# A two-block transformer/Mamba kernel: half of a causal convolution moves from VectorE to TensorE in the last two sequences, with two small moves beside it

## The chip, the cores and the metric

The kernel runs on one core of a Trainium2 chip. The metric is the time of one execution on the device, in microseconds (us). Several executions are timed and the median is taken. One execution is also recorded by the hardware profiler, and all readings below come from that record. TensorE is called PE (PEld is its weight load), VectorE DVE, ScalarE ACT, GpSimd POOL and SyncE SP.

## The reference, cut to what matters

Two blocks run one after the other on an input of 4 sequences, 256 tokens and 512 features, in float32. The first is attention plus a gated feed-forward network. The second normalizes and then adds a selective scan (Mamba) and a mixture of low-rank experts. The change touches the Mamba part only (`d` is one of 1024 channels, `n` one of 16 states):

```python
x, z = split(hidden @ in_proj_w)              # each [b, l, d], transposed to [b, d, l]
xc = conv_b + sum(conv_w[:, k] * xpad[:, :, k : k + 256] for k in range(4))
xc = silu(xc)
dt, B, C = projections of xc, each through an rmsnorm; dt also through softplus
h[t] = exp(dt[t] * A) * h[t-1] + dt[t] * B[t] * xc[t]      # per channel and state
y[t] = sum over n of h[t, n] * C[t, n]
out = ((y + D * xc) * silu(z)) @ out_proj_w
```

## The kernel before

**Layout.** Channels lie on the 128 partitions, so 1024 channels are 8 chunks of 128. Chunks are handled in pairs (`p` = 0 to 3), a pair's two products filling one PSUM tile of 2 x 256 float32 called `px`. The 16 states of a chunk are taken four at a time: one "unit" of the scan stage is 4 states of one chunk, laid out as 128 x 1024: 32 channels x 4 states on the partitions, and 4 such groups of 256 time steps side by side. There are 4 units to a chunk, 32 to a sequence and 128 in all.

**A unit.** In program order unit `u` does: `decays(u + 2)` on ACT, four exponentials of 128 x 255 (L888); then whatever the plan has put at unit `u`; `scan_in(u)` on DVE, the product `bx` (L894); now and then `close_chunk` on DVE, which reads the finished PSUM sum `ysum` of a chunk and multiplies it with the gate (L929); `scan(u)`, the recurrence `h` on DVE (L909) and after it the product `hc` of `h` with C on POOL (L913); and last `states_sum(u - 1)` on PE, which adds the states of the unit before into `ysum` (L923, L925). The last unit alone is scanned in four quarters (`parts=4`, L1277).

**Buffers that tie the engines together.** There are three decay tiles, so `decays(u + 2)` waits for `scan(u - 1)`. There are two `h` tiles, so `scan(u)` waits for the POOL product `hc(u - 2)`. There are three `hc` tiles, so `hc(u)` waits for `states_sum(u - 3)`. `ysum` is a single bank: `close_chunk` at the second unit of a chunk waits for the sum of the last unit of the chunk before. PSUM tiles named `mm` (three of them) hold `px`, the gates' products `pz`, the outputs `po` and small ones in turn.

**The plan.** The order is written out by hand: `put(b, s, f, ...)` (L1141) calls `f` at unit `s` of sequence `b`, and each engine runs its instructions in that order. While sequence `b` is scanned, the next sequence `nxt = b + 1` is prepared. For `nxt` = 2 and 3 the products `px_mm` of pair `p` stand at units 6 + 2p and 7 + 2p, `conv_in` at 8 + 2p, `conv_taps` at 9 + 2p, `conv_silu` at 16; for `nxt` = 1 all are one unit later (L1205 to L1218). After that come `pp_mm` and `pp_norm` (the projections, up to `nrm`, L754), `step_in` and `step_exp` (dt on PE and ACT) and `step_out`, `step_x` (POOL). The first sequence's own convolution stands ahead of the units (L1039 to L1061).

**The convolution before.** A convolution of four taps is a sum of four shifted products. `conv_in` (L699) copies `px` into a padded SBUF tile (L704, ACT) and starts both chunks with the last tap and the bias (L707, ACT: first chunk in place in `px`, second chunk into `xc`), then writes the other three taps of the second chunk (L712, ACT). `conv_taps` (L716) adds the first chunk's three taps on DVE (L720) and the second chunk's on POOL (L726):

```python
for k in range(KC - 1):
    nc.vector.scalar_tensor_tensor(
        px[:, 0, :] if k < KC - 2 else xcs[b][:, c, :], pads[p % 2][:, 0, k : k + S],
        vec[:, c, V_CW + k : V_CW + k + 1], px[:, 0, :], ALU.mult, ALU.add,
    )
```

**The gates of the first sequence.** `pz_mm` is four products into a half of `pz` (L857). For sequence 0, pair 1, both halves stand at unit 8 (L1173 to L1175).

Of the kernel before, what the change touches and what calls it, by code (L numbers as in the profile page):

```python
# [8 lines left out]
F32 = mybir.dt.float32  # L9

F32R = mybir.dt.float32r
AF = mybir.ActivationFunctionType
ALU = mybir.AluOpType
# [4 lines left out]
P = 128  # L18
B, S, D = 4, 256, 512
# [6 lines left out]
DIN, NST, KC, RK = 1024, 16, 4, 32  # L26
DC = DIN // P
NE, LR = 8, 16
NG = 4
# [8 lines left out]
V_CW, V_CB, V_DB, V_AL, V_D, V_END = 0, 4, 5, 6, 22, 23  # L38
# [3 lines left out]
def block_kernel(  # L42
# [655 lines left out]

    def conv_in(b, p):  # L699

        px = live["px", b, p]
        if p == 0:
            xcs[b] = (act if b % 3 else w1).tile([P, DC, S], F32, tag=f"xc{b % 3}", name="xc")
        nc.scalar.copy(pads[p % 2][:, :, KC - 1 :], px)  # L704
        for i in range(2):
            v = vec[:, 2 * p + i, :]
            nc.scalar.activation(xcs[b][:, 2 * p + 1, :] if i else px[:, 0, :], px[:, i, :],  # L707
                                 AF.Identity, bias=v[:, V_CB : V_CB + 1],
                                 scale=v[:, V_CW + KC - 1 : V_CW + KC])
        tp = w1.tile([P, KC - 1, S], F32, tag="tap", name="tap")  # L710
        for k in range(KC - 1):
            nc.scalar.activation(tp[:, k, :], pads[p % 2][:, 1, k : k + S], AF.Identity,  # L712
                                 scale=vec[:, 2 * p + 1, V_CW + k : V_CW + k + 1])
        live["tap"] = tp

    def conv_taps(b, p):  # L716

        px, c = live["px", b, p], 2 * p
        for k in range(KC - 1):
            nc.vector.scalar_tensor_tensor(  # L720
                px[:, 0, :] if k < KC - 2 else xcs[b][:, c, :], pads[p % 2][:, 0, k : k + S],
                vec[:, c, V_CW + k : V_CW + k + 1], px[:, 0, :], ALU.mult, ALU.add,
            )
        xc = xcs[b][:, c + 1, :]
        for k in range(KC - 1):
            nc.gpsimd.tensor_tensor(xc, xc, live["tap"][:, k, :], ALU.add)  # L726
# [172 lines left out]
    def scan(u, parts=1):  # L899
        b, c, g = u // PER, u % PER // NU, u % NU  # L900
        da, bx = live.pop(("da", u)), live["bx"]
        if u < len(lent["h"]):
            h, hc = lend("h", u), lend("hc", u)
        else:
            h = act.tile([P, NG, S], F32, tag="h", name="h", bufs=2)
            hc = act.tile([P, NG, S], F32, tag="hc", name="hc", bufs=3)
        for k in range(parts):
            n = slice(k * NG // parts, (k + 1) * NG // parts)
            nc.vector.tensor_tensor_scan(  # L909
                h[:, n].rearrange("p n t -> p (n t)"), da[:, n].rearrange("p n t -> p (n t)"),  # L910
                bx[:, n].rearrange("p n t -> p (n t)"), 0.0, ALU.mult, ALU.add,
            )
            nc.gpsimd.tensor_tensor(  # L913
                hc[:, n], h[:, n],
                crows[b][:, g, :].unsqueeze(1).to_broadcast([P, NG // parts, S]), ALU.mult,
            )
        live["hc", u] = hc
# [223 lines left out]
    def put(b, s, f, *a):  # L1141
        at.setdefault(b * PER + s, []).append((f, a))
# [5 lines left out]
    for b in range(B):  # L1148
        nxt = b + 1
        if b:  # L1150
            put(b, 0, b_rows, b, 1)
            put(b, 0, spread, "du", b, 1)

            for c in range(DC):
                put(b, c // 2, out_mm, b - 1, 1, c)
            put(b, 3, out_x, b - 1, 1)
            put(b, 4, dense, b - 1, 0, 0)
            put(b, 5, dense, b - 1, 0, 1)
            put(b, 5, expert_out, b - 1, 0)
            for c in range(DC):  # L1160
                put(b, 6 + c, out_mm, b - 1, 0, c)
            put(b, 15, out_x, b - 1, 0)
        else:
            put(b, 1, one_out, 2)
            put(b, 1, one_step, 3)
            put(b, 2, one_out, 3)
            put_late(b, 2, load_z, b, 0)
            put_late(b, 2, lambda: send("dt", 0, 1, dts[0, 0][:, 2:4, :]))
            put_late(b, 2, step_x, b, 1)
            put(b, 4, load_z, b, 1)  # L1170
            for k, n in enumerate(("rl", "bw", "lb", "ow")):
                put(b, 9 + 2 * k, load_late, n)
            for p, u in ((0, 3), (1, 8)):  # L1173
                for i in range(2):
                    put(b, u, pz_mm, b, p, i)  # L1175
            put(b, 4, gate_silu, b, 0)
            put(b, 12, gate_silu, b, 1)
            put_late(b, 1, add_last, 5)
            put_late(b, 3, add_last, 6)
            put_late(b, 4, add_last, 7)  # L1180
        if b:
            put(b, 0, gate_silu, b, 0, 1)

        o = 0 if b else 3
        put(b, 1 if b else 5, step_in, b, 1, 0)
        put(b, 2 if b else 6, step_in, b, 1, 1)
        put(b, 3 if b else 7, step_exp, b, 1)
        for q in range(2):
            for k in range(3):
                put(b, 5 + o + 3 * q + k, step_out, b, 1, q, k)  # L1190
        for p in (2, 3):
            put(b, 3 * p + 2 + o, step_x, b, p)
        for c in range(2, DC):
            o = 0 if b or c < 4 else 1
            put(b, 3 if c == 2 and not b else 4 * c - 6 + o, spread, "dt", b, c)
            put(b, 4 * c - 4 + o, spread, "du", b, c)
        put(b, 10, load_z, b, 2)
        put(b, 12, load_z, b, 3)
        for p, at_i, at_g in ((2, (14, 15), 16), (3, (19, 21), 23)):
            for i in range(2):  # L1200
                put(b, at_i[i], pz_mm, b, p, i)
            if p == 3 or nxt == B:
                put(b, at_g, gate_silu, b, p)
        if nxt < B:
            o = 0 if b else 1  # L1205
            put(b, 0 if b else 2, norm_stats, nxt)
            put(b, 2 if b else 4, norm_scale, nxt)
            put(b, 3 if b else 5, norm_turn, nxt, 0)
            (put if b else put_late)(b, 4 if b else 5, norm_copy, nxt, 0)
            put(b, 4 if b else 5, norm_turn, nxt, 1)  # L1210
            (put if b else put_late)(b, 5, norm_copy, nxt, 1)
            for p in range(NP):
                put(b, 2 * p if b else (5, 6, 9, 9)[p], load_x, nxt, p)
                for i in range(2):
                    put(b, 6 + o + 2 * p + i, px_mm, nxt, p, i)
                put(b, 8 + o + 2 * p, conv_in, nxt, p)
                put(b, 9 + o + 2 * p, conv_taps, nxt, p)
            put(b, 16 + o, conv_silu, nxt, (b, 2))  # L1218
            put(b, 17 + o, pp_mm, nxt, 0)
            put(b, 18, pp_mm, nxt, 1)  # L1220
            put(b, 19, pp_square, nxt)
            put_late(b, 20, pp_norm, nxt)
            put(b, 21, step_in, nxt, 0, 0)
            put(b, 22, step_in, nxt, 0, 1)
            put(b, 22, c_rows, nxt, 0)
            put(b, 23, step_exp, nxt, 0)
            put(b, 23, c_rows, nxt, 1)
            for q in range(2):
                for k in range(3):
                    put(b, 24 + 3 * q + k, step_out, nxt, 0, q, k)  # L1230
            put(b, 27, step_x, nxt, 0)
            put(b, 27, spread, "dt", nxt, 0)
            put(b, 29, spread, "du", nxt, 0)
            put(b, 30, step_x, nxt, 1)
            put(b, 30, b_rows, nxt, 0)
            put(b, 31, spread, "dt", nxt, 1)
            put(b, 23, load_z, nxt, 0)
            put(b, 25, load_z, nxt, 1)
            for k, u in enumerate((27, 28, 29, 31)):
                put(b, u, pz_mm, nxt, k // 2, k % 2)  # L1240
            if b % 2 == 0:
                for i, u in enumerate((16, 17, 18, 20)):
                    put(b, u, router, b, i)
                put(b, 22, route_exp, b)
                put(b, 24, route, b)
            put(b, 25, expert_turn, b)
            put(b, 25, dense, b, 1, 0)
            put(b, 26, dense, b, 1, 1)
            put(b, 27, expert_out, b, 1)
        else:  # L1250

            put(b, 12, expert_turn, b)
            put(b, 17, dense, b, 0, 0)
            put(b, 18, dense, b, 0, 1)
            put(b, 18, expert_out, b, 0)
            put(b, 20, dense, b, 1, 0)
            put(b, 21, dense, b, 1, 1)
            put(b, 21, expert_out, b, 1)
# [138 lines left out]
```

## Time and profile before

| what | value |
|---|---|
| time, median of 4 runs | 887.55 us (887.29 to 891.42) |
| the profiled execution's own time | 887.29 us |
| its span, first to last instruction | 885.5 us |
| busy: PE, DVE, ACT, POOL | 751.2, 685.5, 526.0, 489.9 us |
| DVE: recurrence `h` L909, product `bx` L894 | 288.0 us in 129, 157.6 us in 128 |
| DVE: taps L720 | 14.4 us in 30 and 7.2 us in 15 |
| POOL: `hc` L913, taps L726 | 301.9 us in 131, 32.7 us in 45 |
| PE: `px` L696, 256 instructions | 65.6 us, 405 ns each |

The page has one line per group of instructions: the line of the code, the engine, the operation, the tiles written and read, how often, the time busy and the idle time just before, with what ended it. The timeline gives single instructions (start, length), and windows give the busy time of every engine in a stretch. A matmul in float32 shows as two instructions. The time of an execution is some 2 us longer than its span (887.29 against 885.5); times in the timeline count from the span's start.

### The profile page before, as it was taken

To read this page: it belongs to the slowest core of one execution; us is meant where nothing else is said; L and a number is where in the kernel's file an instruction comes from. 1 tells how busy PE (TensorE), PEld (TensorE's weight loads), DVE (VectorE), ACT (ScalarE), POOL (GpSimd) and SP (SyncE) were. 2 spreads that over 40 slices of the span, in tenths; PEclk is the share of its full clock that TensorE was granted. 3 is DMA by queue.
4 is the path that set the end of the run, shared out by engine and by line. 5 is a ranking of instruction groups with operands and counts; after the bars stand their busy time and mean duration, and the time that the engine had idled before them with its cause. 6 is when DMAs were issued, how large, how long until landed. Compare 5 with 4: busy or idle time off the path is not lost.

```text
span 885.5 us, 10460 instructions
## 1 busy us (share of the span) xinstructions
PE 751.2 (85%) x3554; PEld 430.3 (49%) x3554; DVE 685.5 (77%) x675; ACT 526.0 (59%) x1009; POOL 489.9 (55%) x377
## 2 busy tenths in 40 slices
PE   5999989999989999997797798678898777967975
PEld 3675545667556576664453344334444443422421
DVE  4695553477565333878999999999999999999996
ACT  4225446312536437778777687776786795764561
POOL 4222222001223242748967879869789759797664
PEclk9999999999999999999996999888999889997998
DMA  6232242001112241365832545442546231436200
GB/s 214 60 95 72 72 119 71 13 1 36 48 48 72 72 116 26 96 175 169 238 97 60 155 131 142 109 122 68 167 120 178 78 101 52 129 93 174 77 24 24
DMA packets 67343, 86.67 MB, mean 98 GB/s; under 512 B 12077, under 2 KB 52025, under 8 KB 66906
## 3 DMA queue, kind: packets, MB, share of 16 engines
q1 hardware_dynamic: 57930, 67.12, 26.9%
q0 software_dynamic: 9072, 18.35, 7.5%
q8 instruction: 28, 0.46, 0.2%
q10 hardware_dynamic: 288, 0.52, 0.2%
q14 instruction: 25, 0.20, 0.1%
HBM read 66.58 MB, written 10.22 MB: 87 GB/s over the span
## 4 chain that ended last, share of the span: by engine, by line
PE 40%; DVE 35%; ACT 13%; issue 5%; POOL 4%; DMA 2%; SPq 0%; DVEq 0%; POOLq 0%; ACTq 0%
DVE h L909 20%; DVE bx L894 7%; ACT decay L888 6%; PE po L442 5%; PE pu L417 5%; PE pg L417 4%; PE sc L329 4%; PE av L371 3%; POOL hc L913 3%; PE scT L361 3%; PE pp L740 2%; PE po L1017 2%; PE pz L857 1%; ACT pe L363 1%; PE px L696 1%
## 5 line engine op out<-in xcount | busy, mean ns | idle before, releaser
L913 POOL TENSOR_TENSOR hc<-h,cr 128x1024 f32<-128x1024 f32 (+1 forms) x131 | 301.9, 2307 | 99.5 <-DVE h L909 80.7
L909 DVE TENSOR_TENSOR_SCAN h<-decay,bx 128x1024 f32<-128x1024 f32 (+1 forms) x129 | 288.0, 2234 | 15.6 <-PE po L442 3.9
L888 ACT ACTIVATE decay<-dts,aneg 128x255 f32<-128x255 f32 x504 | 213.5, 498 | 118.2 <-DVE h L909 107.9
L894 DVE TENSOR_TENSOR bx<-brow,dus 128x1024 f32<-128x1024 f32 x128 | 157.6, 1231 | 3.7
L925 PE MATMUL ysum<-hc,stack 128*32 128x256 f32 x1024 | 90.1, 420 | 82.1 <-POOL hc L913 81.6
L429 POOL TENSOR_TENSOR hlo<-g,hhi 128x512 fp32r<-128x512 f32 x28 | 36.1, 1290 | 150.0 <-ACT hhi L428 150.0
L331 DVE TENSOR_REDUCE mpl<-sc 128x4 f32<-128x1024 f32 x64 | 77.2, 1223 | 23.8 <-PE sc L329 23.5
L925 PEld LDWEIGHTS ysum<-hc,stack 128*32 128x32 f32 x1024 | 21.4, 112 | 145.2 <-POOL hc L913 128.1
L400 POOL DMA_DIRECT2D wgu<-in_wgu x56 | 31.2, 557 | 90.9 <-PE pg L417 80.2
L363 ACT ACTIVATE pe<-scT 128x1024 f32<-128x1024 f32 x64 | 62.8, 1023 | 30.1 <-PE scT L361 29.8
L1017 PE MATMUL po<-ow,xc 128*128 128x512 f32 x128 | 72.1, 673 | 2.2 <-DVE xc L929 2.2
L696 PE MATMUL px<-xn1T,w_in 128*128 128x256 f32 x256 | 65.6, 405 | 1.1 <-DMA w_in<-in_inx 1.0
L857 PE MATMUL pz<-xn1T,w_in 128*128 128x256 f32 x256 | 66.0, 404 | 0.0
L696 PEld LDWEIGHTS px<-xn1T,w_in 128*128 128x128 f32 x256 | 51.1, 203 | 20.3 <-issue 9.3
L425 DVE SCALAR_TENSOR_TENSOR g<-g,pg 128x512 f32<-128x512 f32 x28 | 19.2, 685 | 52.0 <-ACT g L424 52.0
L857 PEld LDWEIGHTS pz<-xn1T,w_in 128*128 128x128 f32 x256 | 47.8, 195 | 17.8 <-issue 11.2
L428 ACT CAST hhi<-g 128x512 fp32r<-128x512 f32 x28 | 17.3, 620 | 63.0 <-DVE g L427 62.7
L417 PE MATMUL pg<-xhi,wgu 128*128 128x512 f32 x112 | 46.7, 417 | 7.0 <-issue 4.4
L417 PE MATMUL pu<-xhi,wgu 128*128 128x512 f32 x112 | 47.7, 426 | 2.0 <-DMA wgu<-in_wgu 0.9
L442 PE MATMUL po<-wd,hhi 128*128 128x512 f32 x112 | 48.5, 433 | 0.0
L329 PE MATMUL sc<-km,qg 128*128 128x512 f32 x128 | 44.0, 424 | 3.3 <-ACT pe L363 2.8
L417 PE MATMUL pg<-xlo,wgu 128*128 128x512 f32 x112 | 44.9, 400 | 0.0
(225 smaller groups left out, 1252.9 us busy)
## 6 DMA issues: line engine op xcount, KB each, us to landing
dts<-dtd SPq DMA_DIRECT2D x124, 128.0 KB, 2.8
dus<-dud SPq DMA_DIRECT2D x124, 128.0 KB, 3.0
wgu<-in_wgu POOLq DMA_DIRECT2D x56, 256.0 KB, 2.7
w_in<-in_inz SPq DMA_DIRECT2D x16, 512.0 KB, 4.7
w_in<-in_inx SPq DMA_DIRECT2D x15, 512.0 KB, 4.4
dtd<-dt SPq DMA_DIRECT2D x15, 256.0 KB, 2.2
dud<-du SPq DMA_DIRECT2D x15, 256.0 KB, 2.3
wd<-in_wd POOLq DMA_DIRECT2D x7, 512.0 KB, 3.5
```

The source lines that it names most:

```text
L329: mm(sc[:, hp, :], lhsT=qs[b][:, gq, hf, qb * P : (qb + 1) * P], rhs=kms[b][:, 2 * hp : 2 * hp + 2, :], start=True, stop=True)
L331: nc.vector.tensor_reduce(mpl2[b % 2][:, qb, :, 16 + 2 * gq + hf].rearrange("p (a i) -> p a i", a=2), sc.rearrange("p a (i k) -> p a i k", ...
L417: mm(ps, lhsT=wgus[i][:, hc, :], rhs=xs[j][:, hc, :], start=(hc == 0 and j == 0), stop=(hc == HC - 1 and j == 1))
L442: mm(po, lhsT=hids[th][j][:, m, i * P : (i + 1) * P], rhs=wd[:, m, :], start=False, stop=(m == MC - 1 and j == 1))
L696: mm(px[:, i, :], lhsT=w[:, i, hc, :], rhs=xns[b][:, hc, :], start=(hc == 0), stop=(hc == HC - 1))
L857: mm(pz[:, i, :], lhsT=w[:, i, hc, :], rhs=xns[b][:, hc, :], start=(hc == 0), stop=(hc == HC - 1))
L888: nc.scalar.activation(da[:, k, 1:], live["dts", b, c][:, k, 1:], AF.Exp, scale=aneg[:, c, k, g : g + 1])
L894: nc.vector.tensor_tensor(bx, brow[g // 2][:, g % 2, :].unsqueeze(1).to_broadcast([P, NG, S]), live["dus", b, c], ALU.mult)
L909: nc.vector.tensor_tensor_scan(h[:, n].rearrange("p n t -> p (n t)"), da[:, n].rearrange("p n t -> p (n t)"), bx[:, n].rearrange("p n t -> ...
L913: nc.gpsimd.tensor_tensor(hc[:, n], h[:, n], crows[b][:, g, :].unsqueeze(1).to_broadcast([P, NG // parts, S]), ALU.mult,)
L925: mm(ysum[k * NB : (k + 1) * NB, :], lhsT=stack, rhs=hc[:, k, :], start=False, stop=(g == NU - 1))
L1017: mm(live["po", b, i], lhsT=xcs[b][:, c, i * P : (i + 1) * P], rhs=late_w["ow"][:, c, :], start=False, stop=(c == DC - 1))
```

## The change

Three edits:

1. In `conv_in` and `conv_taps`, for sequences 2 and 3 (`b >= 2`) the first chunk of each pair is convolved by PE. ACT writes four 128 x 128 diagonal matrices (the identity scaled by a tap's weight per channel) into a new tile `dg`; PE multiplies each with the shifted padded input and accumulates all four taps into `px[:, 0]`, over the plain product, which has been copied by then; ACT then adds the bias on the way to `xc`. The three DVE products and the starting ACT product of that chunk go. For sequences 0 and 1 the arithmetic stays, but the starting ACT product of the first chunk now stands after the second chunk's product and its three taps, no longer ahead of them.
2. In the last, quartered unit the fourth quarter's product with C moves from POOL to DVE. In all other units there is one part (`k` = 0), so nothing changes there.
3. For sequence 0, pair 1, the two halves of the gates' product stand at units 6 and 7 in place of both at unit 8.

```diff
     def conv_in(b, p):
...
         nc.scalar.copy(pads[p % 2][:, :, KC - 1 :], px)
-        for i in range(2):
-            v = vec[:, 2 * p + i, :]
-            nc.scalar.activation(xcs[b][:, 2 * p + 1, :] if i else px[:, 0, :], px[:, i, :],
-                                 AF.Identity, bias=v[:, V_CB : V_CB + 1],
-                                 scale=v[:, V_CW + KC - 1 : V_CW + KC])
+        v = [vec[:, 2 * p + i, :] for i in range(2)]
+        nc.scalar.activation(xcs[b][:, 2 * p + 1, :], px[:, 1, :], AF.Identity,
+                             bias=v[1][:, V_CB : V_CB + 1], scale=v[1][:, V_CW + KC - 1 : V_CW + KC])
         tp = w1.tile([P, KC - 1, S], F32, tag="tap", name="tap")
         for k in range(KC - 1):
             nc.scalar.activation(tp[:, k, :], pads[p % 2][:, 1, k : k + S], AF.Identity,
-                                 scale=vec[:, 2 * p + 1, V_CW + k : V_CW + k + 1])
+                                 scale=v[1][:, V_CW + k : V_CW + k + 1])
         live["tap"] = tp
+        if b < 2:
+            nc.scalar.activation(px[:, 0, :], px[:, 0, :], AF.Identity, bias=v[0][:, V_CB : V_CB + 1],
+                                 scale=v[0][:, V_CW + KC - 1 : V_CW + KC])
+        else:
+            dg = live["dg"] = w1.tile([P, KC, P], F32, tag="dg", name="dg")
+            for k in range(KC):
+                nc.scalar.activation(dg[:, k, :], ident, AF.Identity, scale=v[0][:, V_CW + k : V_CW + k + 1])
 
     def conv_taps(b, p):
         px, c = live["px", b, p], 2 * p
-        for k in range(KC - 1):
-            nc.vector.scalar_tensor_tensor(
...
+        if b < 2:
+            for k in range(KC - 1):
+                nc.vector.scalar_tensor_tensor(
...
+        else:
+            for k in range(KC):
+                mm(px[:, 0, :], lhsT=live["dg"][:, k, :], rhs=pads[p % 2][:, 0, k : k + S],
+                   start=(k == 0), stop=(k == KC - 1))
+            nc.scalar.activation(xcs[b][:, c, :], px[:, 0, :], AF.Identity,
+                                 bias=vec[:, c, V_CB : V_CB + 1])
...
-            nc.gpsimd.tensor_tensor(
+            (nc.vector if k == NG - 1 else nc.gpsimd).tensor_tensor(
                 hc[:, n], h[:, n],
...
-            for p, u in ((0, 3), (1, 8)):
+            for p, us in ((0, (3, 3)), (1, (6, 7))):
                 for i in range(2):
-                    put(b, u, pz_mm, b, p, i)
+                    put(b, us[i], pz_mm, b, p, i)
```

More of the change, by code (lines that the diff above doesn't have):

```diff
@@ L712, in conv_in @@
             nc.scalar.activation(tp[:, k, :], pads[p % 2][:, 1, k : k + S], AF.Identity,
[L713 removed]
+                                 scale=v[1][:, V_CW + k : V_CW + k + 1])
         live["tap"] = tp
+        if b < 2:
[5 more added lines that the diff above has]
+                nc.scalar.activation(dg[:, k, :], ident, AF.Identity, scale=v[0][:, V_CW + k : V_CW + k + 1])
     def conv_taps(b, p):
         px, c = live["px", b, p], 2 * p
[L719 to L723 removed]
+        if b < 2:
+            for k in range(KC - 1):
+                nc.vector.scalar_tensor_tensor(
+                    px[:, 0, :] if k < KC - 2 else xcs[b][:, c, :], pads[p % 2][:, 0, k : k + S],
+                    vec[:, c, V_CW + k : V_CW + k + 1], px[:, 0, :], ALU.mult, ALU.add,
+                )
+        else:
[4 more added lines that the diff above has]
+                                 bias=vec[:, c, V_CB : V_CB + 1])
         xc = xcs[b][:, c + 1, :]
```

## The prediction, made before the changed kernel was run

> **What bounds the kernel now.** I read the page's busy row and slices first, then the timeline of single instructions for DVE, POOL, ACT and PE around the convolutions, and last the busy time by stretches.
>
> ```profile
> PE 751.2 (85%) x3554; PEld 430.3 (49%) x3554; DVE 685.5 (77%) x675; ACT 526.0 (59%) x1009; POOL 489.9 (55%) x377
> DVE  4695553477565333878999999999999999999996
> ```
>
> PE has the largest sum, but from the nineteenth slice (about 400 us) on DVE is at 9 in nearly every slice: the scan stage is a DVE queue. A unit without extras takes it 3.69 us (product 1.23, recurrence 2.29 and gaps). So DVE work taken out there looks like time gained, if nothing else is nearly as full. The stretches say what else is. Both hold the eight units with taps, of sequence 1 and of sequence 2; columns are the length, then busy PE, PEld, DVE, ACT, POOL:
>
> ```profile
> 533.30:568.00 34.70, 26.69 (x140) 15.59 (x138) 33.66 (x30) 24.70 (x58) 33.29 (x26) 0.94 0.56 150
> 660.10:694.80 34.70, 28.06 (x149) 16.68 (x147) 33.66 (x30) 24.70 (x58) 33.28 (x26) 0.95 0.53 150
> ```
>
> POOL is busy 33.3 of 34.7 us just there, since it adds the other chunk's taps (3 x 0.73 a pair) and the steps of dt beside its 2.36 us product `hc`. None of that is removed. Four pairs without DVE taps can therefore gain 1.4 us a sequence, not the four times 1.28 that DVE sheds.
>
> **Edit 1, sequences 2 and 3 (prepared in sequences 1 and 2).** What DVE drops, first pair in sequence 2 (start, length):
>
> ```profile
> 662.32 0.99 DVE L720 SCALAR_TENSOR_TENSOR px<-pad,vec,px 128x256 f32<-128x256 f32 x2
> 663.34 0.48 DVE L720 SCALAR_TENSOR_TENSOR xc<-pad,vec,px 128x256 f32<-128x256 f32 x1
> 663.74 1.23 DVE L894 TENSOR_TENSOR bx<-brow,dus 128x1024 f32<-128x1024 f32 x1
> 664.87 0.42 DVE L929 TENSOR_TENSOR xc<-ysum,sz 128x256 f32<-128x256 f32 x1
> 665.21 2.28 DVE L909 TENSOR_TENSOR_SCAN h<-decay,bx 128x1024 f32<-128x1024 f32 x1
> ```
>
> Such a unit takes 5.09 us (660.12 to 665.21) or, without the L929 line, 4.96 (668.85 to 673.81); without taps 3.80 and 3.68. That is 1.28 a pair, 8 x 1.28 = 10.2 us in all, the edit's full promise. What POOL and PE say (sequence 2):
>
> ```profile
> 669.49 2.34 POOL L913 TENSOR_TENSOR hc<-h,cr 128x1024 f32<-128x1024 f32 x1
> 676.57 2.33 POOL L726 TENSOR_TENSOR xc<-xc,tap 128x256 f32<-128x256 f32 x3
> 678.86 4.69 POOL L913 TENSOR_TENSOR hc<-h,cr 128x1024 f32<-128x1024 f32 x2
> 681.27 0.64 PE L925 MATMUL ysum<-hc,stack 128*32 128x256 f32 x8 [0.93 <-POOL hc L913]
> ```
>
> POOL runs without a gap from 655.17 to 688.14, so these times stay. First pair: the recurrence at 665.21 comes 1.28 earlier. Second: the one at 673.81 would come 2.57 earlier, but its `h` tile is free only when the `hc` of 669.49 ends (671.8): 1.9 earlier. Third: `close_chunk` (682.22) needs the sum whose `hc` ends at 681.2 and which PE adds from 681.27 to 681.91; the recurrence of 682.55 then starts at about 682.3, 0.25 earlier. Fourth: 0.25 + 1.28 = 1.5 earlier. So 1.5 us is gained by the end of the taps, by POOL's leave.
>
> What is added. PE: 4 products a pair, 8 instructions, 1.82 from the first one's start to the next work's, as eight `px` ones take (659.66 to 661.48). That is 7.3 us a sequence, against 34.7 - 28.1 = 6.6 us idle in the stretch. It fits only since most of it falls in waits for POOL (2.40 us before 671.88), and since such a gap is followed by slow products (2.94 us for eight at 674.05, against 1.89; granted clock 0.91 there); filled, I expect the full clock. With it PE has done its list at 680.4, before the 681.27 sum needs it. ACT: it loses a 0.54 product and gains four diagonals and one 0.56 product from PSUM. The diagonals are not in the trace; by the 128x136 copy (0.27) and the 128x256 tap (0.40 apart) they cost 1.1 to 1.6 a pair; I take 1.2, the nearer in size. ACT idles about 2.5 us a pair, so this is hidden; without cover it would be 1.2 a pair.
>
> The new wait: ACT's last product waits for PE, and behind it on ACT stand the decays, and for the fourth pair `conv_silu`. PE reaches the fourth pair's products after the sum of the `hc` that ends at 688.14, its list of two gates' products (1.9 each) and the four new ones: about 693.7. ACT is then free at 694.3, does a decay (1.7) and starts the table load at 696.0 instead of 695.20: silu 0.75 late, although DVE is 1.5 early. In sequence 2 PE has no gap from silu to `nrm` (13.00 busy of 13.00 us from 699 to 712), and `nrm` started at 711.98 with the recurrence before it ended at 711.95, no slack. So the gain is lost there: -1.5 if that chain gives way, +0.75 if it holds; I take **+0.4**, near the chain. In sequence 1, without the router's products, `nrm` (585.11) has 1.8 us of slack behind its input (583.3); 1.4 survives, of which PE's gates' product standing ahead of `pdt`, and POOL's next full stretch (601 to 627, opened by ACT's step), let through about **-0.9** (ends -1.5 and 0).
>
> **Edit 1, sequences 0 and 1.** Arithmetic stays, order does not. Before:
>
> ```profile
> 406.17 0.56 ACT L704 COPY pad<-px 128x512 f32<-128x512 f32 x1
> 406.76 0.54 ACT L707 ACTIVATE px<-px,vec 128x256 f32<-128x256 f32 x1
> 407.33 0.56 ACT L707 ACTIVATE xc<-px,vec 128x256 f32<-128x256 f32 x1
> 407.80 1.29 ACT L712 ACTIVATE tap<-pad,vec 128x256 f32<-128x256 f32 x3
> 407.93 1.01 DVE L720 SCALAR_TENSOR_TENSOR px<-pad,vec,px 128x256 f32<-128x256 f32 x2 [1.89 <-ACT xc L707]
> ```
>
> DVE has already waited 1.89 us here for ACT, which has no gap since 382. Now `xc` comes at 406.76, the taps from 407.23, `px` from 408.42 to 408.96: DVE starts 1.1 later. The second pair: DVE starts at 416.57, 0.2 after ACT's 416.38, so it will wait 0.9; ACT's part there is paced by the recurrence of the first pair (its decay waits for that), so the delays add. Third (it waited 0.35): +0.4 more, since ACT's row was full. Fourth: +0.9. Sum **+3.3**; ends 0 (DVE waits for something else) and 4 x 1.1 = 4.4. DVE is full from there to the end, so nothing takes it back. In the lead-in the same order frees `px` 1.1 later and holds up the fourth pair's products by about 0.3 (335.33 instead of 335.01), on the chain: **+0.3** (0 to 0.3).
>
> **Edit 3.** PE is without a gap from 393.2 to 405.7, so the sum at 402.72, for which `close_chunk` waited 1.17, comes after the same work as before. And the next unit waits for ACT anyway. Gain 0; `pdt` now stands behind the first half, up to 0.3 for ACT; I take **+0.1**.
>
> **Edit 2.** At the end:
>
> ```profile
> 873.21 5.08 POOL L913 TENSOR_TENSOR hc<-h,cr 128x1024 f32<-128x1024 f32 x5 [1.33 <-DVE h L909]
> 879.00 0.42 DVE L929 TENSOR_TENSOR xc<-ysum,sz 128x256 f32<-128x256 f32 x1 [2.12 <-PE ysum L925]
> ```
>
> The four quarters end 0.68 apart, the last at 878.29. DVE is free at 876.9 and does the quarter in 0.43 (the row of `du`, L1096), so POOL's third, 877.65, is last: -0.64, less a PE sum that now follows directly: **-0.5** (ends 0 and -0.64).
>
> [...]
>
> **Sum.** 887.29 (the profiled execution; span 885.5) + 0.3 + 3.3 + 0.1 - 0.9 + 0.4 - 0.5 = 890.0. The median of the runs is 0.26 above that execution, well inside the range.
>
> **Rivals.**
> - DVE's whole 10.2 passes: POOL would have to give way, its stretches becoming shorter. 887.29 - 10.2 - 0.5 + 3.7 = 880.3. For it: DVE's row of nines. Against it: 33.3 of 34.7. Chance 0.12.
> - The order costs nothing (DVE's start hangs on the copy alone): 890.0 - 3.6 = 886.4. Against it: the waits end with the second product's end, 407.89. Chance 0.14.
> - Slower: PE falls behind. If half-clock stretches stay (1.05 us each, as at 674.05), PE needs 28.1 + 7.3 = 35.4 us in 34.7; the 681.27 sum and so `close_chunk`, and ACT's wait for PE, come late. It decides from where PE's list passes 681.3, 0.9 us after my 680.4. Then each of the two sequences loses about 0.7 + 1.05 + 0.75 = 2.5 instead of my -0.9 and +0.4: 890.0 + 5.5 = 895.5. Chance 0.19.
> - The forecast, 888 to 892: 0.55.
>
> **Numbers.** The bounds of the unknown terms reach from 884 (order free, both sequences' POOL-limited gains) to 895 (PE behind). What is below holds most of the first rival's chance, above about half of the third's: 0.2. A measurement of this kernel can tell about 0.5% (4.4 us): faster 0.12; same, the order rival and most of the forecast, 0.66; slower 0.22.
>
> **What would show it.** Right: in sequences 1 and 2 POOL without a gap through the stretch, DVE with gaps ahead of the recurrences there that end on POOL or PE; in sequence 0 DVE's waits at L726 of about 3, 0.9, 0.8 and 0.9 us, ended by ACT's `px`; silu no earlier relative to the fourth pair; three quarters on POOL. Wrong: units of 3.7 us straight through the stretch, or no added waits in sequence 0.

## The result, and the profile after

The changed kernel takes 892.58 us (median of 53 runs, 889.25 to 896.99), the kernel before 889.33 us (79 runs, 884.98 to 895.81). The ratio is 1.0032, 95% interval 1.002 to 1.0043: 2.9 us slower, between 1.8 and 3.8. The forecast was 2.7 us slower (890.0 against its profiled execution of 887.29). In these runs the kernel before took 889.33 us itself, not 887.29, so the difference is what is compared, not the 890.0. Two of the 12 executions of e1 below took 1073.53 us (the profiled one, at a mean granted clock of 0.64) and 1415.8 us, so they and its trace are left out of the comparison. The profiled execution of the kernel after took 893.32 us (span 891.5), 6.0 us more than that of before; why this one pair differs by twice what the medians do is part of what follows.

The page of after, the row of busy times and DVE's slices:

```profile
PE 764.4 (86%) x3618; PEld 443.4 (50%) x3618; DVE 676.9 (76%) x652; ACT 532.0 (60%) x1041; POOL 489.2 (55%) x376
DVE  5695554377564323976989999899998989999996
```

DVE is busy 8.6 us less (676.9 for 685.5) in a span 6 us longer: what it shed became waiting. PE took on 13.2 us, ACT 6.0. The busy time by stretches shows where DVE waits; these are the same eight units of sequences 1 and 2 that the prediction showed at 34.70 us (length, then PE, PEld, DVE, ACT, POOL, granted clock):

```profile
540.47:573.72 33.25, 30.83 (x163) 20.38 (x162) 28.72 (x18) 26.81 (x69) 32.36 (x26) 1.00 0.48 140
665.78:699.07 33.29, 30.91 (x165) 20.73 (x163) 28.72 (x18) 26.80 (x69) 32.39 (x26) 1.00 0.49 143
```

DVE went from 33.66 to 28.72, the length only from 34.70 to 33.25: POOL, 32.36 of 33.25, now holds it. The timeline shows the two places in sequence 1 (in brackets the idle time before and what ended it):

```profile
552.23 2.29 DVE L921 TENSOR_TENSOR_SCAN h<-decay,bx 128x1024 f32<-128x1024 f32 x1 [0.74 <-POOL hc L926]
559.22 4.68 POOL L926 TENSOR_TENSOR hc<-h,cr 128x1024 f32<-128x1024 f32 x2
561.62 0.64 PE L938 MATMUL ysum<-hc,stack 128*32 128x256 f32 x8 [0.88 <-POOL hc L926]
562.33 0.42 DVE L942 TENSOR_TENSOR xc<-ysum,sz 128x256 f32<-128x256 f32 x1 [2.86 <-PE ysum L938]
```

The wait of 2.86 us names PE, but PE itself had waited 0.88 us for POOL: the chain is POOL, then one sum, then `close_chunk`.

To see where each microsecond went, take the start of the same recurrence in two traces; the difference is the shift, and it changes only where something changed. After minus before: +0.44 at unit 8; +5.80 at unit 16 (sequence 0's taps); +7.11 at unit 24 (behind `nrm`); +5.67 behind sequence 1's convolution; +4.25 behind sequence 2's; +5.41 behind its `nrm`, and so to the end.

In sequence 0 two things meet:

```profile
393.67 3.78 PE L869 MATMUL pz<-xn1T,w_in 128*128 128x256 f32 x8 [0.42 <-ACT dt L797]
398.78 0.47 ACT L796 ACTIVATE u<-pdt,vec 128x256 f32<-128x256 f32 x1 [2.61 <-PE pdt L791]
406.09 0.42 DVE L942 TENSOR_TENSOR xc<-ysum,sz 128x256 f32<-128x256 f32 x1 [3.40 <-PE ysum L938]
412.01 1.01 DVE L726 SCALAR_TENSOR_TENSOR px<-pad,vec,px 128x256 f32<-128x256 f32 x2 [3.30 <-ACT px L715]
```

The first half of the second gates' products stands ahead of `pdt` on PE and ran at the half clock (3.78 us for eight, at a granted clock of 0.50 from 393.67 to 397.45; the same eight take 1.99 in e11 at 398.74, at 1.00). ACT waited 2.61 us for `pdt`, and its full row of work was late by that. PE's list has no gap from 393.67 on, so it was late too, and with it a sum and a `close_chunk`. The last line is the order of ACT's products: DVE's first tap waits for `px`.

### The profile page after: what moved, and what is told of

It is laid out like the page before. It is cut to its first block, busy times and chain, and to the rows that moved or that the text cites. A ratio compares the mean times of both kernels' runs of the same rounds, so it can differ in the third digit from the quotient of the medians.

```text
span 891.5 us, 10609 instructions
## 1 busy us (share of the span) xinstructions
PE 764.4 (86%) x3618; PEld 443.4 (50%) x3618; DVE 676.9 (76%) x652; ACT 532.0 (60%) x1041; POOL 489.2 (55%) x376
## 4 chain that ended last, share of the span: by engine, by line
PE 40%; DVE 32%; ACT 13%; POOL 6%; issue 6%; DMA 1%; DVEq 0%; ACTq 0%; POOLq 0%
DVE h L921 20%; ACT decay L900 7%; DVE bx L906 6%; PE po L442 5%; PE pu L417 5%; PE pg L417 4%; PE sc L329 4%; PE av L371 3%; POOL hc L926 3%; PE scT L361 3%; PE pz L869 2%; PE px L696 2%; PE pp L752 2%; PE ysum L938 1%; ACT pe L363 1%
## 5 line engine op out<-in xcount | busy, mean ns | idle before, releaser
L869 PE MATMUL pz<-xn1T,w_in 128*128 128x256 f32 x256 | 69.7, 420 | 0.4 <-ACT dt L797 0.4
L696 PE MATMUL px<-xn1T,w_in 128*128 128x256 f32 x256 | 62.5, 390 | 1.5 <-DMA w_in<-in_inx 0.7
L869 PEld LDWEIGHTS pz<-xn1T,w_in 128*128 128x128 f32 x256 | 50.3, 206 | 20.5 <-issue 9.9
L696 PEld LDWEIGHTS px<-xn1T,w_in 128*128 128x128 f32 x256 | 48.8, 194 | 17.0 <-issue 7.6
```

Source lines behind the costliest of these rows:

```text
L696: mm(px[:, i, :], lhsT=w[:, i, hc, :], rhs=xns[b][:, hc, :], start=(hc == 0), stop=(hc == HC - 1))
L869: mm(pz[:, i, :], lhsT=w[:, i, hc, :], rhs=xns[b][:, hc, :], start=(hc == 0), stop=(hc == HC - 1))
```

## The experiments

The runs of each kernel (12, of e6 9) leave intervals about 0.5% wide, some 5 us; what one part does is less than that, so the shifts in the traces decide, and the times say whether they add up. The table gives the change of the shift over four pieces, where the unit numbers count from the first recurrence, and the time from the last recurrence's start to the last `close_chunk`; the time is the median, beside the ratio to the kernel before in the same rounds.

| kernel | us | ratio, 95% interval | units 8 to 20 | 40 to 54 | 64 to 82 | 82 to 86 | last |
|---|---|---|---|---|---|---|---|
| before | | | | | | | 4.54 |
| after | 892.58 | 1.0032 (1.002 to 1.0043) | +5.35 | -1.44 | -1.41 | +1.16 | 4.58 |
| e1, old order | 890.93 | 1.0018 (0.9994 to 1.0042) | | | | | |
| e2, gates whole | 891.88 | 1.0033 (1.001 to 1.0057) | +2.61 | -1.28 | -1.42 | +2.43 | 4.57 |
| e3, quarter on POOL | 893.09 | 1.004 (1.0013 to 1.0067) | +3.34 | -1.33 | -1.40 | +2.38 | 4.97 |
| e4, PE part alone | 888.84 | 0.9997 (0.9971 to 1.0023) | +1.34* | -1.21 | -1.41 | +2.46 | 4.98 |
| e5, order alone | 893.81 | 1.0032 (1.0003 to 1.0061) | +3.33 | 0 | 0 | -0.14 | 4.98 |
| e6, PE, no POOL taps | 884.72 | 0.9936 (0.9909 to 0.9964) | 0 | -3.18 | -3.92 | +1.16 | 4.97 |
| e7, no POOL taps | 889.85 | 1.0007 (0.9975 to 1.0039) | +1.81* | 0 | 0 | -0.14 | 4.97 |
| e8, three pairs | 890.36 | 1.0006 (0.9981 to 1.0031) | +3.41* | -0.49 | -0.68 | +0.19 | 4.98 |
| e9, two pairs | 889.85 | 0.999 (0.9962 to 1.0017) | 0 | -0.29 | -0.40 | 0 | 4.55 |
| e10, first pair | 889.96 | 0.9999 (0.9968 to 1.003) | 0 | -0.21 | -0.18 | -0.13 | 4.53 |
| e11, gates alone | 889.61 | 0.999 (0.9958 to 1.0022) | +0.69 | +0.20 | 0 | -0.13 | 4.97 |
| e12, two pairs, later | 890.22 | 0.9986 (0.9963 to 1.0008) | +1.90* | +0.49 | +0.23 | -0.13 | 4.98 |

A star marks a shift in a piece where that kernel issues just what the kernel before issues: it is put down to the clock's phase of that execution (last section), and it is the measure of how far one trace can be trusted in that piece. The stars reach 3.4 us, more than any part of the change, so a step counts here only where several traces repeat it. The pieces left out of the table move too without an edit in them: units 54 to 64 take 1.4 us longer in e5, e8, e10 and e11 than in before.

**e1: the order undone** (in the kernel after).

```
         v = [vec[:, 2 * p + i, :] for i in range(2)]
+        if b < 2:
+            nc.scalar.activation(px[:, 0, :], px[:, 0, :], AF.Identity, bias=v[0][:, V_CB : V_CB + 1],
+                                 scale=v[0][:, V_CW + KC - 1 : V_CW + KC])
...
         live["tap"] = tp
-        if b < 2:
-            nc.scalar.activation(px[:, 0, :], px[:, 0, :], AF.Identity, bias=v[0][:, V_CB : V_CB + 1],
-                                 scale=v[0][:, V_CW + KC - 1 : V_CW + KC])
-        else:
+        if b >= 2:
```

> The kernel after, but for sequences 0 and 1 ACT's product of px stands ahead of the one of xc again, as before. My theory (the order makes DVE wait at its first tap): the forecast's 3.3 + 0.3 = 3.6 us goes, so about 0.3 us below the kernel before, with DVE's waits of 0.9 to 3.3 us at the taps of sequence 0 back at 1.9 and under. By the traces' own sum (+0.4 lead-in, +3.1 in units 10 to 16, part of it caused by the late second gates) 3 to 3.5 us goes. Rival (the order costs nothing, the waits only take the place of others): it stays 3.2 us above the kernel before.

Measured: 1.0018, interval 0.9994 to 1.0042, which holds both -0.3 and +3.2 us. It decides nothing; e5 asks the same from the other side.

**e2: the gates' products whole again** (in the kernel after).

```
-            for p, us in ((0, (3, 3)), (1, (6, 7))):
+            for p, u in ((0, 3), (1, 8)):
```

> The kernel after, but the second gates' products of sequence 0 stand together in unit 8 again. My forecast costs that edit at 0.1 us, so no change (3.1 us above the kernel before). The theory that the traces suggest: the first half now stands ahead of pdt on PE, ACT's row is then 2 us late, and unit 9 of the profiled execution paid 2.2 us for it: 2.2 us less, 1.0 us above the kernel before, the wait of 2.6 us at ACT's first u gone. Between the two: a part of it was only the slow clock phase of that execution, 0.5 to 1.5 us less.

Measured: the time is not told apart from the kernel after (1.0033), the trace is clear. ACT's wait is gone, unit 9 has no shift, and what remains is the order alone, DVE's four waits in sequence 0:

```profile
406.93 1.01 DVE L726 SCALAR_TENSOR_TENSOR px<-pad,vec,px 128x256 f32<-128x256 f32 x2 [2.79 <-ACT px L715]
416.31 1.01 DVE L726 SCALAR_TENSOR_TENSOR px<-pad,vec,px 128x256 f32<-128x256 f32 x2 [0.66 <-ACT px L715]
425.69 1.01 DVE L726 SCALAR_TENSOR_TENSOR px<-pad,vec,px 128x256 f32<-128x256 f32 x2 [0.53 <-ACT px L715]
435.07 1.01 DVE L726 SCALAR_TENSOR_TENSOR px<-pad,vec,px 128x256 f32<-128x256 f32 x2 [0.66 <-ACT px L715]
```

By the shifts they cost 0.90 (2.79 for 1.89), 0.77, 0.18 and 0.77 us, together 2.6. The last three steps repeat within 0.01 us in the kernel after, e3 and e5, and the starred kernels have no step at the second and third pair; the first, 0.90, agrees with e3's 1.63 less the 0.70 of e11.

**e3: the last quarter on POOL again** (in the kernel after).

```
-            (nc.vector if k == NG - 1 else nc.gpsimd).tensor_tensor(
+            nc.gpsimd.tensor_tensor(
```

> The kernel after, but the last quarter's product with C is on POOL again. My forecast says that edit gains 0.5 us, so 0.5 us more than the kernel after, 3.7 us above the kernel before. Rival, from the traces: the quarter took 0.90 us on DVE where I had put 0.43, and close_chunk starts 4.58 us after the last recurrence instead of 4.54: no change, within 0.1 us of the kernel after at the same clock phase, and the last chain as long as before (4.5 us from the recurrence to L942).

Measured: from the last recurrence to `close_chunk` 4.97 us, against 4.58 and 4.57 in the two kernels with the quarter on DVE. The first lines are the kernel after's, the second e3's:

```profile
879.87 2.42 DVE L921 TENSOR_TENSOR_SCAN h<-decay,bx 128x256 f32<-128x256 f32 x4
882.40 0.90 DVE L926 TENSOR_TENSOR hc<-h,cr 128x256 f32<-128x256 f32 x1
884.45 0.42 DVE L942 TENSOR_TENSOR xc<-ysum,sz 128x256 f32<-128x256 f32 x1 [1.15 <-PE ysum L938]
```

```profile
877.33 2.42 DVE L921 TENSOR_TENSOR_SCAN h<-decay,bx 128x256 f32<-128x256 f32 x4
882.30 0.42 DVE L942 TENSOR_TENSOR xc<-ysum,sz 128x256 f32<-128x256 f32 x1 [2.56 <-PE ysum L938]
```

In all of these PE ends 1.12 us after the last quarter (in after 883.30 to 884.42, at a granted clock of 0.50), in before 0.67 (878.29 to 878.96, at 1.00): the same eight products, at the half and at the full clock. With the quarter on POOL the distance is 4.97 or 4.98 in eight traces and 4.53 to 4.55 in three, and nowhere between. At one clock, where PE takes 1.12 us in both, the edit gains 0.4 us; that after and before seem equal (4.58 and 4.54) is the clock again. My rival was built on that comparison and falls. The same run says something of the gates: e3 has the new order and the split gates at the full clock (1.00 from 392.79 to 416.69), and its +3.34 is 0.73 above e2's.

**e4: the PE part alone** (the kernel after with the edits of e1, e2 and e3, so that against the kernel before only this is left).

```
+        if b >= 2:
+            dg = live["dg"] = w1.tile([P, KC, P], F32, tag="dg", name="dg")
...
+            for k in range(KC):
+                mm(px[:, 0, :], lhsT=live["dg"][:, k, :], rhs=pads[p % 2][:, 0, k : k + S],
+                   start=(k == 0), stop=(k == KC - 1))
```

> The kernel before with one part of the change alone: in the last two sequences TensorE convolves the first chunk of each pair; sequences 0 and 1 keep their order, the gates' products stay in unit 8, the last quarter on POOL. My theory (POOL is full in those stretches, so its own taps decide): -0.5 us by the forecast (-0.9 and +0.4), -1.7 by the traces (-1.44 and -0.25), with POOL without a gap and DVE waiting about 0.75 and 2.9 us in each stretch. Rival (DVE is the bound, all that it sheds passes): -10.2 us. Rival (PE falls behind): +5 us.

Measured: 0.9997, interval -2.6 to +2.0 us. DVE's whole -10.2 and PE's +5 are both outside it. The stretches are 33.28 and 33.29 us, POOL busy 32.40 in each, and the gain of 1.2 to 1.4 us is there in both sequences. In sequence 2 it is not only lost but overpaid, +2.46 behind the convolution:

```profile
694.82 0.47 ACT L734 ACTIVATE xc<-px,vec 128x256 f32<-128x256 f32 x1 [1.45 <-PE px L732]
696.90 1.28 ACT L741 ACT_TABLE_LOAD   x1
698.19 1.91 ACT L741 ACTIVATE xc<-xc 128x2048 f32<-128x2048 f32 x1
700.15 3.67 PE L752 MATMUL pp<-xc,xpw 128*64 128x256 f32 x8 [2.83 <-ACT xc L741]
714.20 0.48 DVE L766 SCALAR_TENSOR_TENSOR nrm<-pp,lnw,rs 64x256 f32<-64x256 f32 x1 [2.49 <-ACT rs L652]
```

silu's table load comes 1.70 us later than in before, though the sequence was entered only 1.17 later: 0.53 late, behind ACT's product that waits 1.45 us for PE. PE waits 2.83 us for silu, where it waited 1.82 before, and `nrm` ends 2.2 us later than in before: 1.0 net of the entry. About half of that 1.0 is the clock and not the change. These are the stretches from the first `pp` to `nrm` in the kernel before, the kernel after and e4 (length, then PE, PEld, DVE, ACT, POOL, granted clock):

```profile
698.46:711.98 13.52, 13.52 (x72) 8.14 (x73) 12.99 (x8) 8.52 (x21) 8.21 (x4) 0.81 0.27 78
704.64:717.39 12.75, 12.75 (x72) 7.61 (x73) 11.06 (x7) 8.61 (x21) 8.13 (x4) 0.87 0.34 85
700.15:714.20 14.05, 14.05 (x72) 8.55 (x73) 11.06 (x7) 8.51 (x21) 9.41 (x4) 0.78 0.33 77
```

PE has no gap in any of them, and length times granted clock is 11.0 us, within 0.1, in all three. So `nrm` comes when PE's work is done, silu's 0.53 us arrives there in full, and the rest is how much of the stretch fell at the half clock: +0.5 us in e4 (14.05 for 13.52; e2 and e3 have 14.01 and 13.96), -0.8 in the kernel after (12.75). That is why the kernel after shows +1.16 in this piece and e2 and e3, with the same instructions there, +2.4.

**e5: the order alone** (in the kernel before).

```
-        for i in range(2):
+        for i in (1,) if b < 2 else (0, 1):
...
         live["tap"] = tp
+        for i in (0,) if b < 2 else ():
```

> The kernel before with one part of the change alone: in sequences 0 and 1 (and in the lead-in) ACT's product of px stands behind the taps. My theory, the forecast's term: +3.3 (waits at DVE's first taps of sequence 0: 3.0, 0.9, 0.8, 0.9 us) and +0.3 in the lead-in, so +3.6 us. From the traces of two kernels with it and without the slow clock phase (shift of the recurrences from unit 9 to 16: +2.6 and +3.1): +2.6 to +3.5. Rival (the order costs nothing, the earlier loss was the slow clock phase): 0, with the waits at the taps' first instruction as in the kernel before (1.9, 0, 0.35, 0).

Measured: 1.0032, 0.3 to 5.4 us slower; "costs nothing" is just outside. The waits of the second to fourth pair are 0.66, 0.54 and 0.66 us as in e2, and the shift +3.33; of it 1.6 at unit 10 contain the half clock in unit 9 (0.50 from 390.89 to 401.13), so e2's 2.6 is the better figure.

**e6: PE's convolution, and POOL without its taps** (e4, with POOL's loop empty for `b >= 2`).

```
-        for k in range(KC - 1):
+        for k in range(KC - 1 if b < 2 else 0):
             nc.gpsimd.tensor_tensor(xc, xc, live["tap"][:, k, :], ALU.add)
```

> TensorE convolves the first chunk as in the kernel of the part alone (old order, gates in unit 8, last quarter on POOL), and POOL's taps of the other chunk are left out in the last two sequences (that chunk's convolution is then only its last tap and the bias). Theory (POOL held DVE's gain back; the next bound is PE, busy 31.6 to 32.1 of 33.3 us in those stretches): the stretch of eight units goes from 33.3 to about 32 us, so some 1 to 1.5 us a sequence more than with the taps, -2 to -5 us against the kernel before, with waits of DVE for POOL gone. Rival (POOL was the only limit): a stretch of 29.6 us, -10 us. Rival (POOL does not decide): 33.3 us, no difference from the kernel with the taps.

Measured: 0.9936, 3.2 to 8.1 us faster than before. Its stretches:

```profile
534.53:566.04 31.51, 31.51 (x168) 21.27 (x166) 28.72 (x18) 26.67 (x69) 24.91 (x14) 1.00 0.56 154
658.21:688.99 30.78, 30.78 (x165) 20.74 (x163) 28.72 (x18) 26.58 (x69) 24.94 (x14) 1.00 0.57 154
```

With POOL out of the way the gain rises from 1.2 and 1.4 to 3.2 and 3.9 us, and PE is busy every moment of the stretch. DVE's one long wait in each, 1.73 and 0.99 us at a `close_chunk`, is for PE's sum: PE is the next bound, 1.2 to 2.0 us short of the 5.1 (4 x 1.28) that DVE shed.

**e7: POOL without its taps, DVE with its own** (the kernel before with e6's edit).

> The kernel before, with POOL's taps left out in the last two sequences and DVE's kept (that chunk's convolution is then only its last tap and the bias). Theory (before, DVE is the first bound of the stretch, 33.66 busy of 34.7 us, POOL second at 33.3): the stretch becomes 33.7 to 34.7 us, so 0 to -1 us a sequence, 0 to -2 us in all. Rival (POOL alone decides already in the kernel before, its full row paces DVE): several us less, -5 and more.

Measured: 34.70 and 34.71 us, DVE busy 33.66, POOL 24.97, no shift; 1.0007. With e4 and e6 this is a square: DVE's taps away -1.2 to -1.4, POOL's away 0, both away -3.2 to -3.9 a sequence. Before the change DVE held the stretch alone, POOL stood 1.2 to 1.4 us behind it and PE another 2.0 to 2.5 behind that.

**e8: PE takes a chunk in three of the four pairs, one of them POOL's.**

```
+    def on_pe(b, p):
+        return (0, 1, 0, None)[p] if b >= 2 else None
```

> In the last two sequences TensorE convolves one chunk in three of the four pairs: in the first and third the one that DVE had, in the second the one that POOL had; the fourth pair stays as before (old order, gates in unit 8, last quarter on POOL). Theory (both DVE and POOL must give way, and ACT's wait for PE in the fourth pair cost the way to silu): busy time of the stretch 31.1 us on DVE, 31.0 on POOL, about 30 to 32 on PE, so 32.2 to 33 us instead of 34.7, and silu not late: -1.7 to -2.5 us a sequence, -3 to -5 us in all. Rival (the chain silu, pp, nrm pays it back in sequence 2 as with four pairs, +2.4 at the recurrence behind nrm): about -2 us. Rival (POOL does not decide): no better than with four pairs, 0.

Measured: stretches of 33.86 and 34.01 us, and shifts of -0.5 and -0.7: the forecast of 32.2 to 33 fell. POOL has room now (31.23 busy) and is not what this `close_chunk` waits for:

```profile
558.62 0.64 PE L941 MATMUL ysum<-hc,stack 128*32 128x256 f32 x8
559.33 0.42 DVE L945 TENSOR_TENSOR xc<-ysum,sz 128x256 f32<-128x256 f32 x1 [1.29 <-PE ysum L941]
```

The sum stands in PE's list without a gap since 550.19, behind a convolution and eight `px` products; POOL had delivered its input. (PE's own last wait before that, 0.81 us at 550.19, was for POOL.) What did come out is silu: +5.23 later than before, exactly the shift of the recurrences there, and the `nrm` piece costs +0.19 instead of +1.2 to +2.4. So it is ACT's wait for PE in the fourth pair that e4 and the kernel after pay for in sequence 2.

**e9 and e10: two pairs, and the first pair alone.**

```
-        return (0, 1, 0, None)[p] if b >= 2 else None
+        return (0, 1, None, None)[p] if b >= 2 else None
...
+        return (0, None, None, None)[p] if b >= 2 else None
```

> In the last two sequences TensorE convolves DVE's chunk of the first pair and POOL's chunk of the second; third and fourth pair, the order, the gates and the last quarter as before. Theory (POOL is full, so DVE's 1.28 us stays gained only where POOL sheds work too, and silu isn't late when ACT's wait for PE is not in the fourth pair): recurrences 1.3 us earlier from the first pair to the end of each stretch, silu earlier by the same, -1.3 us a sequence, -2.6 us in all. Rival (PE's list is what makes close_chunk late in the third pair, POOL is not): the gain is lost at the third pair as with three pairs, -0.5 us a sequence, about -1 us.

> As in the kernel with two pairs, but only DVE's chunk of the first pair is on TensorE; POOL keeps all its taps. Theory (POOL full): the first pair's recurrence 1.3 us earlier, and at the third pair's close_chunk all but 0.25 us of it given back, so -0.25 us a sequence, -0.5 us in all, about 2 us more than with two pairs. Rival (POOL doesn't decide): the same as with two pairs.

Measured: e10 is as forecast: 1.29 us earlier at the first pair, 0.2 left at the third, where `close_chunk` waits for PE's sum, and PE had waited 2.42 us for POOL. e9 is not: 1.30 earlier at the first two pairs, 0.29 and 0.40 left at the end. POOL is no longer the cause there; ACT is, which stands still for PE ahead of the third pair's inputs:

```profile
549.61 0.47 ACT L736 ACTIVATE xc<-px,vec 128x256 f32<-128x256 f32 x1 [3.63 <-PE px L734]
553.34 1.01 DVE L728 SCALAR_TENSOR_TENSOR px<-pad,vec,px 128x256 f32<-128x256 f32 x2 [0.63 <-ACT xc L710]
```

**e11: the gates in two steps alone** (in the kernel before).

```
-            for p, u in ((0, 3), (1, 8)):
+            for p, us in ((0, (3, 3)), (1, (6, 7))):
```

> The kernel before with one part of the change alone: the second gates' products of sequence 0 in units 6 and 7. The forecast's term: +0.1 us (0 to 0.3). Theory from the traces with the order changed too (ACT waits for pdt behind the first half, 0.61 us at full clock and 2.61 at the half, and DVE waits for ACT at the first taps in unit 10): +0.7 us at unit 10 at full clock, up to 2 at the half one. Rival (close_chunk's wait of 1.17 us goes with them): -0.5 to -1.6 us, the more the slower the clock is there.

Measured: the time shows nothing (0.999, 0.9958 to 1.0022), the trace 0.70 us at unit 10, at the full clock (1.00 from 394.58 to 418.47) and with nothing else changed. Its lines:

```profile
398.27 0.47 ACT L784 ACTIVATE u<-pdt,vec 128x256 f32<-128x256 f32 x1 [0.58 <-PE pdt L779]
405.59 0.42 DVE L929 TENSOR_TENSOR xc<-ysum,sz 128x256 f32<-128x256 f32 x1 [1.37 <-PE ysum L925]
410.59 1.02 DVE L720 SCALAR_TENSOR_TENSOR px<-pad,vec,px 128x256 f32<-128x256 f32 x2 [2.38 <-ACT xc L707]
```

`close_chunk` waits 1.37 us (1.17 before): nothing is gained. ACT is 0.58 later, and DVE's next wait, which hangs on ACT, is 0.49 longer: with the 0.20 at `close_chunk` that is the 0.70.

**e12: e9, with the second pair's products on PE and ACT's product of them one unit later.**

```
+                if p == 2 and on_pe(nxt, 1) == 1:
+                    put(b, 12, conv_pe, nxt, 1)
```

> The kernel with two pairs, but the second pair's products on TensorE and ACT's product of them come one unit later, behind ACT's inputs of the third pair. Theory (what took the gain back in the third pair is ACT's wait of 3.6 us for those products, which stand on PE behind a sum that waits for POOL): that wait is gone, the recurrence of the third pair keeps the 1.3 us of the first, -1.3 us at the end of each stretch instead of -0.3 to -0.4, -2.6 us in all. Rival (PE's list is full anyway, px of the fourth pair is late instead, since its PSUM slot is that of the second pair): the gain goes at the fourth pair, no better than with two pairs.

Measured: the rival was right. ACT's wait is gone, and the fourth pair's `px` waits for the PSUM slot of the second instead; it holds up the sum behind it on PE, and `close_chunk` waits 1.39 us:

```profile
555.01 1.99 PE L696 MATMUL px<-xn1T,w_in 128*128 128x256 f32 x8 [0.91 <-ACT xc L745]
```

The sequences end 0.49 and 0.23 us later than without. No mixture of these was faster than the kernel before by more than the runs can tell (e12's 0.9986 reaches to 1.0008, though its own trace shows no gain); e6, which leaves work out, isn't one.

## Why the prediction was right

Term by term, in us; the third column is measured on the kernels named, which differ from their partner in that term, at the same clock where there was such a pair.

| term | forecast | measured | from |
|---|---|---|---|
| lead-in | +0.3 | not seen | see below |
| order, sequences 0 and 1 | +3.3 | +2.6 | e2 |
| gates in two steps | +0.1 | +0.7 | e11; e3 less e2 0.7 |
| conv on PE, sequence 1 | -0.9 | -1.2 to -1.4 | e4, after |
| conv on PE, sequence 2 | +0.4 | +0.5 (-0.25 to +1.0 with the clock) | after, e2, e3, e4 |
| last quarter on DVE | -0.5 | -0.4 | e3, e4 against after, e2 |
| sum | +2.7 | about +2.1 (1.4 to 2.6) | runs: +2.9 (1.8 to 3.8) |

The direction and the mechanism of each edit were right; that the sum came so near is partly luck. The order was put 0.7 too high and the gates 0.6 too low, and these two nearly cancel; the gain in sequence 1 was 0.3 to 0.5 larger than taken. Of the 2.9 us of the runs some 0.8 is not in the measured terms; the runs' interval holds both sums.

- **POOL as the limit** was right to the place: the prediction put the four recurrences at 1.3, 1.9, 0.25 and 1.5 us earlier; after shows 1.30, 1.93, 0.24 and 1.47. PE's 0.9 us in hand ahead of the sum in question came out at 0.88, and the filled PE at full clock (1.00 in both stretches).
- **The order** was right in kind, and the waits in the kernel after, 3.30, 0.66, 0.54 and 0.66, stand against the forecast's 3.0, 0.9, 0.8 and 0.9. The sum 3.3 was 0.7 high; the step "DVE starts 1.1 later" failed in size: from the start of ACT's copy to the end of the product that DVE needs it is 2.6 us in the new order (e3: 406.38 to 409.02) and 1.72 in the old, 0.9 later, since ACT's instructions start 0.39 to 0.47 us apart in the new order, while in the old one the copy and the two products start 0.57 to 0.59 apart, each 0.03 us after the end of the one before (406.17, 406.76, 407.33).
- **The gates** are the mis-sized term, at "up to 0.3 for ACT": ACT waits 0.58 to 0.61 us for `pdt`, and since it has no gap from there to DVE's next wait, all of it and a little more arrives. At the half clock it waited 2.61 us (after, 0.50 from 391.07 to 397.90). "Gain 0" was right.
- **Sequence 2**: the prediction gave silu 0.75 late and `nrm` +0.75 "if it holds", and took +0.4, in between. The chain held in all four traces with the edit, the kernel after among them (11.0 us of PE work at the granted clock, under e4), and silu was 0.53 late, so the term is +0.5 at the clock of before. The +0.4 is near that because two errors met: silu was put 0.2 too late, and the chain was allowed to give way, which it did in none of the four. What the clock adds, -0.8 to +0.5 in these four, was no term of the prediction; how often each case comes up is not known.
- **The diagonals**, taken at 1.2 us a pair, took 1.17 (e4: 690.03 to 691.20), and behind them ACT still waited 1.45 us for PE at the fourth pair, so they were hidden there as forecast.
- **The lead-in** can't be judged: recurrence 0 starts between 1.91 us earlier and 1.96 later than in the profiled before, in kernels of the old order (-0.48 to 1.96) as in those of the new one (-1.91 to 0.44).
- **Of the rivals**, DVE's whole 10.2 us is out by e4, "the order costs nothing" by e2's and e5's waits, and PE's falling behind by its idle 0.88 us. PE does become the bound where POOL is relieved (e6).

## What to carry to other kernels

Work taken off the engine that shows the nines passed here only down to the next full row (1.2 to 1.4 of 5.1 us a sequence, to POOL's 32.36 busy of 33.25): read the busy times by stretch, not over the span, and follow the wait one engine further than the one it names (DVE waited for PE, PE for POOL). An instruction added at the end of a chain is priced by what stands behind it in its engine's list: ACT's one product of 0.47 us cost more by its wait for PE (1.45 us in e4, 3.63 in e9) than by its length, and moving it moved the wait to a PSUM slot. When a change is worth less than the spread of the runs, compare where the same instruction starts in two traces, and look first for pieces that should not differ at all. Where PE works without a gap, multiply the length of the stretch by its granted clock before comparing (11.0 us in all three stretches under e4, whose lengths were 12.75 to 14.05).

## What the hardware showed that I had not expected

**TensorE's granted clock fell after windows that were partly busy, and where they lay moved the profile by nearly as much as the change does (2.5 of the profiled pair's 6.0 us, against 2.9 in the runs).** Cut into windows of 3.41 us from the right start, all 13 traces show a granted clock of 1.00 or 0.50 in every window from 342 to 655 us, and nothing between. Three neighbouring windows in the kernel before (PE's busy time follows the length, the granted clock is the third figure from the end):

```profile
543.05:546.46 3.41, 1.33 (x10) 0.64 (x11) 3.34 (x5) 3.38 (x9) 3.41 (x3) 1.00 0.00 0
546.46:549.88 3.42, 3.42 (x9) 2.37 (x7) 3.28 (x3) 0.94 (x4) 3.42 (x3) 0.50 0.75 219
549.88:553.29 3.41, 3.41 (x20) 1.98 (x18) 3.31 (x3) 3.34 (x8) 3.25 (x4) 1.00 0.85 222
```

The half clock came for one window after one that was busy 1.33 of 3.41 us, with no gap above 2.41 us. In the 13 traces, from 342 to 655 us, all 64 windows at the full clock that were busy less than 0.44 of their length were followed by one at the half clock. The share alone does not sort them: 55 of the 122 falls there came after a window that was busy 0.45 or more, 25 of them after 0.6 or more, and what decided there is not known. The eight products at 674.05 that the prediction gives with a clock of 0.91 had 0.64 (674.05 to 676.99; 0.91 is the mean of 672 to 690). Where the windows begin differed from run to run, and with it which piece was slow: ahead of sequence 0's first taps the clock was 0.50 from 389.45 to 392.86 in before, from 395.64 to 399.05 in e4. In e7, which up to sequence 1 issues just what the kernel before does, it was 0.50 from 390.21 to 400.45, on PE's work ahead of sequence 0's unit 9, and these products start at 400.47 instead of 397.34:

```profile
400.47 3.72 PE L857 MATMUL pz<-xn1T,w_in 128*128 128x256 f32 x16
406.55 0.42 DVE L929 TENSOR_TENSOR xc<-ysum,sz 128x256 f32<-128x256 f32 x1 [4.79 <-PE ysum L925]
```

`close_chunk` waited 4.79 us instead of 1.17, and the recurrence came 3.6 us late, of which 1.6 stayed. Sequence 0's own way from `pp` to `nrm` (units 20 to 24) shows it again: 10.33 us in before and 11.64 in after, at a granted clock of 0.85 and 0.76, so 8.8 us in both when multiplied by it. So much of the profiled pair's 6.0 us is the clock: 2.0 us in units 8 to 20 (5.35 against e3's 3.34 with the same instructions), 1.3 in units 20 to 24, and -0.8 in sequence 2. That the runs' spread of 11 us comes from it too is likely (of the 29 executions of before in the rounds of e11 the shortest, 884.99 us, had a mean granted clock of 0.939, the longest, 897.48 us, 0.920), but was not tried.

**DVE and POOL side by side.** The last quarter took DVE 0.90 us (882.40 to 883.30 in after) while POOL was busy on its own for 0.62 of it, where the same shape took 0.43 with POOL idle (before, 354.60); POOL's quarters still came 0.68 apart, each 0.72 to 0.74 long. POOL's third quarter had started 0.11 us earlier, at 882.29; DVE took 0.47 longer than the 0.43 that the prediction put, and POOL's quarter no longer than its others. Why DVE was slower there was not tried. The edit gained 0.4 us all the same, since POOL's fourth quarter would have been later still (4.97 us to `close_chunk` in e3, against 4.58).
